# A graph attention layer on one core: edge ids worked beside the first k,v rows, and k,v split into bf16 pieces in PSUM

## The chip, the cores and the metric

The kernel runs on one core of one Trainium2 chip. Its time is the device time of one execution in microseconds (us), from the first to the last instruction and what lies around them; lower is better. In what follows PE is TensorE (the matmul engine), PEld its weight loads, DVE is VectorE, ACT is ScalarE, POOL is GpSimd, and SP is SyncE, which issues most DMAs. All of them run at once; each takes its own instructions strictly in order.

## The reference

One layer of graph attention with 12500 nodes and 412500 edges, sorted by destination `dst`, followed by two layer norms. With `q`, `k`, `v`, `h` linear in the node features and `eh` linear in the edge features:

```
attn_in = concat([q[src], k[tgt], eh])                      # src, tgt are the edge's two ends
hmid    = leaky_relu(attn_in @ A1 + b1);  scores = leaky_relu(hmid @ A2 + b2)
w       = softmax(scores.mean(-1), axis=0)                  # over all edges
out     = segment_sum(w[:, None] * v[tgt], src)
x       = layernorm(x + (gamma * layernorm(h + out) + beta))
```

A1 is folded into the weights of q, k and eh, so that an edge's hidden row is a sum of three rows.

## The kernel before

**Two streams.** The edges are taken in 403 groups of 1024 (8 tiles of 128), in the order of the sorted `dst`. Stream one, `make(p)`, turns each tile of 128 edges into 128 records of 260 floats: the k row plus the edge part, the v row, and the place of the edge's other end. A record is written to a table in DRAM (`rtab`), at the place that puts edges with like `src` together. Stream two, `sums_of`, reads blocks of that table back, computes scores, weights and weighted sums, and the tail of the program does the two norms (`closing`). The edges are cut into three parts (groups 0 to 73 are not yet followed by any sums; from group 74 on both streams run side by side).

**Making records.** For each group: two one-hot matrices on DVE (`onehots`, which writes `oh`, `few` and `ohd`), two small counts on PE (`count`), the records' places on DVE (`masked`, `places`, the last writes `idx`); then for each half group 4 tiles of matmuls into one PSUM tile `pkv` (`rows`, lines 931 and 936: the first picks k,v rows out of 128 rows `kvs`, the second adds the edge part), a copy by ACT to one of 6 buffers `rec` (`evacuate`, lines 946 and 947), and four indirect DMAs issued by POOL (line 958). A group is thus 8 such DMAs, and there are 3224 in all. The loads of a group stand four groups ahead in SP's queue (`load`, `load_ids`).

**The tables that this needs.** `kvs` comes from a DRAM table `kvtab`, where each of the 98 blocks of 128 node rows holds k and v as three bf16 pieces whose sum is the float32 value (s=0 is the value rounded to bf16, s=1 the rounded remainder, s=2 the remainder of that). The first 7 blocks (`NB`) are made at the start, the other 13 lots of 7 by the generator `tables()` in small steps between the steps of `make`; the same generator then makes 14 lots of q and h rows. A lot of k,v: a load of `xt`, 7 matmuls into PSUM tiles `ph`, 7 additions of the bias on DVE into an SBUF tile `ns` (line 1731), then `parts3`: ACT copies to bf16 (line 1694), DVE subtracts that copy from the float32 (line 1699), ACT, DVE, ACT; then one DMA to `kvtab`. The ids of the edges (`edges`: `dI`, `sI`; results `dtab`, `stab` and `start`, `blk`, `srcl`, `twin`) are made likewise in chunks: the first has 104 groups and is made at the start, the six others of up to 52 by the generator `later()`.

**What sets the order.** From `with tc.manual_schedule()` on the order is the one written: a loop over the steps `i` of `make` (6 to a group) takes a step of `tables()` whenever `made * n0 < i * nt` and one of `later()` whenever `sent * n0 < i * ne`. n0 is nine tenths of the steps of the first 74 groups (399), nt the number of steps that `tables()` has, ne that of `later()`. Before that point, the start, a list scheduler orders what the program has written. In the kernel before the start runs: weights (`first_layer`), the first k,v rows, their split (lines 628 and 631, all on DVE), the write to `kvtab` (line 633), and then the first chunk of ids, whose buffers come from a pool that is opened after the pool of the first rows is closed.

Of the kernel before, what the change touches and what calls it, by code (L numbers as in the profile page):

```python
# [10 lines left out]
FP = mybir.dt.float32  # L11
BF = mybir.dt.bfloat16
# [9 lines left out]
P = 128  # L22
D = 128
DE = 64
H = 8
# [356 lines left out]
def first_layer(nc, prep, pprep, WqT, WkT, WeT, Wv, Wn, A1, bq, bk, be, bv, bn, b1):  # L382

    A1s = prep.tile([D, 3, D], FP)
    nc.sync.dma_start(out=A1s, in_=A1.rearrange("(s k) d -> k s d", k=D))
    wT = prep.tile([D, 2, D], FP)
# [5 lines left out]
    cols = prep.tile([D, 3], FP)  # L392
    for i, b in enumerate((bq, bk, be)):
        nc.sync.dma_start(out=cols[:, i : i + 1], in_=b)
    W = prep.tile([D, 4, D], FP)
    nc.sync.dma_start(out=W[:, 2, :], in_=Wv)
    nc.sync.dma_start(out=W[:, 3, :], in_=Wn)
    bias = prep.tile([P, 4, D], FP)
    nc.vector.memset(bias[:, 1, :], 0.0)
    nc.sync.dma_start(out=bias[:, 2, :], in_=bv.to_broadcast([P, D]))  # L400
    nc.sync.dma_start(out=bias[:, 3, :], in_=bn.to_broadcast([P, D]))
    b1_b = prep.tile([P, D], FP)
    nc.sync.dma_start(out=b1_b, in_=b1.to_broadcast([P, D]))
# [68 lines left out]
def sorted_path(  # L472
# [39 lines left out]
    A2s = const.tile([D, 32], FP)  # L512
    nc.vector.memset(A2s, 0.0)
    nc.scalar.dma_start(out=A2s[:, :H], in_=A2)
    nc.vector.tensor_reduce(A2s[:, H : H + 1], A2s[:, :H], AX.X, ALU.add)
    for j, part in enumerate((1.0, -1.0)):
        nc.vector.tensor_scalar(
            A2s[:, H + 1 + j : H + 2 + j], A2s[:, H : H + 1], part * SLOPE / (1 - SLOPE), None,
            op0=ALU.mult,
        )  # L520
    nc.vector.memset(A2s[:, H : H + 1], 0.0)
    b2_r = const.tile([1, 32], FP)
    nc.vector.memset(b2_r, 0.0)
    nc.scalar.dma_start(out=b2_r[:, :H], in_=b2.rearrange("h o -> o h"))
    nc.vector.tensor_reduce(b2_r[:, H : H + 1], b2_r[:, :H], AX.X, ALU.add)
    for j, part in enumerate((1.0, -1.0)):
        nc.vector.tensor_scalar(
            b2_r[:, H + 1 + j : H + 2 + j], b2_r[:, H : H + 1], part * SLOPE / (1 - SLOPE), None,
            op0=ALU.mult,
        )  # L530
    nc.vector.memset(b2_r[:, H : H + 1], 0.0)
    b2_d = dram.tile([32, 1], FP, name="b2_d")
    nc.scalar.dma_start(out=b2_d.rearrange("h o -> o h"), in_=b2_r)
    b2_c = const.tile([P, 1], FP)
    headsum = const.tile([P, 4], FP)
    nc.vector.memset(headsum, 0.0)
    signs = const.tile([32, 1], FP)
    nc.gpsimd.memset(signs, 1 - SLOPE)
    nc.gpsimd.affine_select(
        out=signs, in_=signs, compare_op=ALU.not_equal, fill=SLOPE - 1, base=-(H + 2),  # L540
        pattern=[[0, 1]], channel_multiplier=1,
    )
    for j in range(4):
        nc.scalar.dma_start(out=b2_c[32 * j : 32 * j + 32, :], in_=b2_d)
        nc.vector.tensor_copy(headsum[32 * j : 32 * j + 32, j : j + 1], signs)


# [48 lines left out]
    def kv_product(xt, pool, j):  # L596
        pn = pool.tile([P, 4 * P], FP, name="ph")
        nc.tensor.matmul(
            pn[:, : 2 * D], xt[:, j, :], Wkv.rearrange("k s d -> k (s d)"), start=True, stop=True
        )  # L600
        return pn

    def kv_biased(ns, j, pn):
        nc.vector.tensor_add(
            ns[:, j, :, :], pn[:, : 2 * D].rearrange("p (s d) -> p s d", s=2), bias_kv
        )
# [5 lines left out]
    with tc.tile_pool(name="prep", bufs=1) as prep, tc.tile_pool(  # L612
        name="pprep", bufs=1, space=PSUM
    ) as pprep, tc.tile_pool(name="pnode", bufs=4, space=PSUM) as pnode:
        W, We_, bias = first_layer(
            nc, prep, pprep, WqT, WkT, WeT, Wv, Wn, A1, bq, bk, be, bv, bn, b1
        )
        nc.vector.tensor_copy(Wkv, W[:, 1:3, :])
        nc.vector.tensor_copy(bias_kv, bias[:, 1:3, :])
        xt = prep.tile([D, NB, P], FP, name="xt")  # L620
        nc.sync.dma_start(out=xt, in_=xN[:, 0, :, :])
        ns = prep.tile([P, NB, 2, D], FP, name="ns")
        for j in range(NB):
            kv_biased(ns, j, kv_product(xt, pnode, j))
        skv = prep.tile([P, NB, 3, 2, D], BF, name="skv")
        rest = ns
        for s in range(3):
            nc.vector.tensor_copy(skv[:, :, s, :, :], rest)
            if s < 2:
                less = prep.tile([P, NB, 2, D], FP, name=f"less{s}")  # L630
                nc.vector.tensor_tensor(less, rest, skv[:, :, s, :, :], op=ALU.subtract)
                rest = less
        nc.sync.dma_start(out=kv_rows(0), in_=skv.rearrange("p b s t d -> p (b s t d)"))
        nc.vector.memset(WeS, 0.0)
        for h in range(2):
            half = slice(h * DE, (h + 1) * DE)
            nc.vector.tensor_copy(WeS[half, h, :], We_[half, :])
        for to, of in ((Wqh, W), (bias_qh, bias)):
            nc.vector.tensor_copy(to, of[:, 0:4:3, :])

# [14 lines left out]
    def edges(tmp, c, size):  # L655
# [22 lines left out]
        yield  # L678
        nc.vector.tensor_reduce(mm[:m, 0, c : c + 1], dl[:m, :], AX.X, ALU.max)
        yield  # L680
        nc.vector.tensor_reduce(mm[:m, 1, c : c + 1], dl[:m, :], AX.X, ALU.min)
        nc.sync.dma_start(out=start[:, g0:g1], in_=stab[g0:g1, :].rearrange("g o -> o g"))
# [34 lines left out]
    with tc.tile_pool(name="tmp", bufs=1) as tmp:  # L717
        for _ in edges(tmp, 0, CH):
            pass

# [982 lines left out]
    def tables():  # L1703
# [10 lines left out]

        load_x(0)
        yield
        for i, (kv, g) in enumerate(jobs):
            load_x(i + 1)
            xt = xts.pop(i)
            ns = np_.tile([P, NB, 2, D], FP, name=f"ns{i % 2}")  # L1720
            w, bias = (Wkv, bias_kv) if kv else (Wqh, bias_qh)
            for j in range(NB + 1):
                before = ph if j else None
                if j < NB:
                    ph = php.tile([P, 4 * P], FP, name="ph")
                    nc.tensor.matmul(
                        ph[:, : 2 * D], xt[:, j, :], w.rearrange("k s d -> k (s d)"),
                        start=True, stop=True,
                    )
                if j:  # L1730
                    nc.vector.tensor_tensor(
                        ns[:, j - 1, :, :].rearrange("p s d -> p (s d)"), before[:, : 2 * D],
                        bias.rearrange("p s d -> p (s d)"), op=ALU.add,
                    )
                yield
            sp = np_.tile([P, NB, 3, 2, D], BF, name="sp")
            if kv:
                yield from parts3([sp[:, :, s, :, :] for s in range(3)], ns, 2)
                nc.sync.dma_start(
                    out=kv_rows(g), in_=sp.rearrange("p b s t d -> p (b s t d)")  # L1740
                )
                made_rows[0] = g + 1
            else:
                sq = np_.tile([P, NB, 2, 1, D], HF, name="sq")
                yield from powers(g, ns[:, :, 0, :])
                yield from parts3([sq[:, :, s, :, :] for s in range(2)], ns[:, :, 0:1, :], 1)
                bl = slice(g * NB, (g + 1) * NB)
                nc.sync.dma_start(out=htab[:, bl, :], in_=ns[:, :, 1, :])
                nc.sync.dma_start(
                    out=qtab[:, bl, :], in_=sq.rearrange("p b s o d -> p b (s o d)")  # L1750
                )
# [27 lines left out]
    with tc.manual_schedule():  # L1779
# [12 lines left out]
        tabs, made, nt = tables(), 0, 1 + (2 * ng - 1) * (NB + 7) + ng  # L1792
# [119 lines left out]
```

## Time and profile before

| | us |
|---|---|
| median of 3 runs | 4827.88 (4826.07 to 4830.85) |
| the profiled execution, whole time | 4829.19 |
| its span, first to last instruction | 4827.2 |
| first indirect DMA of a record starts | 59.30 |
| last one starts | 4282.75 |

The profile's page has a share of busy time by engine (DVE 84%, PE 83%, POOL 68%, ACT 65% over the span). These are averages over a start (to 59 us), a first stage in which only records and tables are made (to about 860), a long stage with both streams (to 4284), and a tail without records. So stages are read apart below. Rows of the group views have busy time in us and mean nanoseconds of one instruction after the first bar, and the idle time of the engine before them, with what ended it, after the second. Rows of the timeline begin with the start and the length in us. Rows of the windows give for a stretch its length, then busy time and the count of instructions, the granted clock of PE as a share, the busy share of the DMA engines and GB/s.

### The profile page before, as it was taken

How to read it: one execution, taken by the hardware profiler on the slowest of the kernel's cores; microseconds unless marked ns; L12 is line 12 of the kernel's file. 1: busy time of each engine (PE TensorE's matmuls, PEld its weight loads, DVE VectorE, ACT ScalarE, POOL GpSimd, SP SyncE). 2: the span in 40 equal slices, each digit the busy share in tenths (PEclk: the TensorE clock that was granted, in tenths of full speed). 3: DMA queues.
4: the chain of work that ended last, by engine and by line, in shares of the span. 5: the costliest groups of instructions: out<-in, count | busy, mean ns of one | idle time of the engine just before them, and what ended most of it. 6: DMA issues, size and time to landing. Idle time of an engine off the chain costs nothing. (4 is left out here: it accounts for less than half of the span.)

```text
span 4827.2 us, 84360 instructions
## 1 busy us (share of the span) xinstructions
PE 3991.6 (83%) x26680; PEld 3111.2 (64%) x26680; DVE 4064.7 (84%) x8217; ACT 3144.8 (65%) x8198; POOL 3304.4 (68%) x3279
## 2 busy tenths in 40 slices
PE   3556655577788999999999999998998899998997
PEld 2334433466666777777777666666777777666777
DVE  8878886688878999999998888888999988877767
ACT  2432222366666778787787777777777777777886
POOL 3777777777777777777777777777777777741103
PEclk7877785899888999999999999999999999999999
DMA  6888887888988999999999999999999999989964
GB/s 196 282 279 288 286 298 243 294 300 298 296 299 299 358 336 334 333 348 337 323 335 324 329 331 329 332 336 325 342 332 326 333 316 334 320 294 327 318 215 176
DMA packets 599153, 1484.41 MB, mean 308 GB/s; under 512 B 100352, under 2 KB 299923, under 8 KB 596902
## 3 DMA queue, kind: packets, MB, share of 16 engines
q1 hardware_dynamic: 436350, 1049.04, 65.4%
q0 software_dynamic: 154752, 429.39, 23.3%
q8 instruction: 212, 3.47, 0.3%
q14 instruction: 247, 2.02, 0.1%
q10 hardware_dynamic: 7592, 0.48, 0.1%
HBM read 906.61 MB, written 611.06 MB: 314 GB/s over the span
## 5 line engine op out<-in xcount | busy, mean ns | idle before, releaser
L958 POOL DMA_INDIRECT rtab<-rec,idx x3224 | 3219.2, 999 | 1061.2 <-issue 777.2
L946 ACT ACTIVATE rec<-pkv 128x1024 f32<-128x1024 f32 x806 | 822.2, 1020 | 1120.4 <-DMA rtab<-rec,idx 572.8
L1346 ACT ACTIVATE ohw<-ohs,w 128x128 f32<-128x128 bf16 x3626 | 1189.1, 399 | 75.7 <-DVE ohs L1332 27.2
L1375 PE MATMUL psm<-rt,ohw 128*128 128x128 f32 x7252 | 1023.1, 285 | 1.1 <-ACT ohw L1346 1.0
L1375 PEld LDWEIGHTS psm<-rt,ohw 128*128 128x128 f32 x7252 | 943.9, 197 | 76.1 <-ACT hm L1243 7.7
L936 PE MATMUL pkv<-WeS,eat 128*128 128x256 f32 x3224 | 946.4, 421 | 0.0
L1247 DVE TENSOR_TENSOR hm<-ph,hm 128x512 f32<-128x512 f32 (+1 forms) x949 | 627.4, 661 | 300.9 <-ACT hm L1243 299.0
L931 PE MATMUL pkv<-kvs,ohd 128*128 128x256 bf16 x3224 | 539.1, 295 | 373.6 <-ACT rec L946 370.2
L931 PEld LDWEIGHTS <-ohd 128*128 128x128 bf16 x3224 | 320.9, 105 | 645.9 <-issue 531.8
L936 PEld LDWEIGHTS pkv<-WeS,eat 128*128 128x128 f32 x3224 | 620.2, 214 | 75.0
L1224 PE MATMUL ph<-ident,rt 128*128 128x128 f32 x3626 | 587.2, 284 | 64.5 <-DVE hm L1247 63.6
L1210 DVE TENSOR_SCALAR ohT<-rowB,iotaP,power 128x512 bf16<-128x512 uint8 (+2 forms) x1274 | 598.9, 492 | 34.8 <-DMA rowB<-row 34.6
L1243 ACT ACTIVATE hm<-ph 128x512 f32<-128x512 f32 (+1 forms) x949 | 537.5, 566 | 84.1 <-PE ph L1233 29.2
L1224 PEld LDWEIGHTS ph<-ident,rt 128*128 128x128 f32 x3626 | 418.3, 146 | 269.7 <-issue 145.5
L1233 PE MATMUL ph<-ohT,qs 128*128 128x512 bf16 (+2 forms) x2548 | 559.7, 323 | 16.1 <-DVE ohT L1210 11.3
L872 DVE TENSOR_SCALAR ohd<-dstb,node 128x1152 bf16<-128x1152 uint8 x404 | 565.0, 1399 | 4.5 <-PE pkv L931 4.5
L900 DVE TENSOR_TENSOR ats<-pc,oh 128x792 f32<-128x792 f32 x403 | 392.2, 973 | 61.7 <-PE pc L880 56.6
L1332 DVE TENSOR_TENSOR ohs<-iotaE,sl 128x512 bf16<-128x512 bf16 (+1 forms) x949 | 404.6, 426 | 5.0 <-ACT ohw L1346 4.8
L862 DVE TENSOR_REDUCE few<-oh 128x99 bf16<-128x792 bf16 x403 | 395.1, 980 | 13.9
L911 DVE TENSOR_REDUCE pos<-ats 128x8 f32<-128x792 f32 x403 | 390.7, 970 | 2.5
L1258 PE MATMUL psc<-hm,A2s 128*32 128x512 f32 (+1 forms) x1898 | 345.9, 607 | 31.9 <-DVE hm L1247 23.7
L1284 PEld LDWEIGHTS psm<-headsum,z 96*128 96x128 f32 (+2 forms) x2112 | 259.7, 193 | 32.8 <-issue 8.3
(190 smaller groups left out, 3790.5 us busy)
## 6 DMA issues: line engine op xcount, KB each, us to landing
rt<-rtab SPq DMA_DIRECT2D x160, 1950.0 KB
rt<-rtab SPq DMA_DIRECT2D x96, 1560.0 KB
eat<-in_ea SPq DMA_DIRECT2D x201, 512.0 KB
rtab<-rec,idx POOLq DMA_INDIRECT x3224
dstb<-dtab SPq DMA_DIRECT2D x201, 256.0 KB
qs<-qtab SPq DMA_DIRECT2D x256, 192.0 KB
atab<-old SPq DMA_DIRECT2D x256, 192.0 KB
old<-atab SPq DMA_DIRECT2D x224, 192.0 KB
```

What stands on the lines that cost most here:

```text
L872: nc.vector.tensor_scalar(to, row[:, cols], node, None, op0=ALU.is_equal)
L931: nc.tensor.matmul(pk[:, i, h, :], ohd[t], kvs, start=(h == 0), stop=False,)
L936: nc.tensor.matmul(pk[:, i, :, :D], eat[:, (j + i) * P : (j + i + 1) * P], WeS, start=False, stop=True,)
L946: nc.scalar.activation(rec[:, :, :, : 2 * D], pk, AF.Copy)
L958: one_tile = nc.gpsimd.indirect_dma_start(out=rtab[p % TABS][:, :], out_offset=bass.IndirectOffsetOnAxis(ap=idxs[g][:, t : t + 1], axis=0) ...
L1210: nc.vector.tensor_scalar(st["oh"][k][:, (a - t0) * P : (b - t0) * P], st["rowB"][:, a * P : b * P], iotaP, power[:, bs[u] : bs[u] + 1], o ...
L1224: nc.tensor.matmul(ph[:, j * P : (j + 1) * P], st["rt"][:, t0 + j, :D], ident, is_transpose=True, start=(j == 0), stop=False,)
L1233: nc.tensor.matmul(ph[:, cols], st["qs"][:, j0 // t, s, :], oh[:, cols], start=False, stop=(s == 1 and j1 == t0 + n),)
L1243: nc.scalar.activation(hm, state[i]["ph", k][:, : n * P], AF.Copy, scale=SLOPE)
L1247: nc.vector.tensor_tensor(hm, ph[:, : n * P], hm, op=ALU.max)
L1346: nc.scalar.activation(ohw[:, j, :], ohs[:, :, j], AF.Copy, scale=st["w"][:, t0 + j : t0 + j + 1])
L1375: nc.tensor.matmul(st["psS"][:, (1 + u) * P : (2 + u) * P], ohw[:, j, :], st["rt"][:, t0 + j, D : 2 * D], start=(k == 0), stop=(k == t - 1),)
```

## The change

Four things, in one edit:

1. **The start in another order.** `edges` and its tiles are defined ahead of the first rows, the pools of both are open together, and the first chunk of ids now has 52 groups (so that seven more follow instead of six). Its loads `dI` and `sI` are the first DMAs of SP. Steps of it are interleaved with the first k,v rows. `first_layer` gives the three columns of biases and the three broadcast biases to ACT's DMA queue (`small`), and its loads are in another order.
2. **k,v split in PSUM.** New `kv_stages`: two blocks of 128 rows share one PSUM tile of 512 floats. `product` (PE), `biased` (DVE adds the bias within PSUM), `piece(0)` (ACT writes the bf16 piece from PSUM), `rest_of(0)` (PE adds minus that piece to the PSUM tile, by a bf16 matmul with minus the identity), `piece(1)`, `rest_of(1)`, `piece(2)`. It serves the first rows and the 13 other lots. DVE's copies and subtractions of lines 628, 631 and 1699 (for k,v) are gone, and so is ACT's one copy of 7 blocks at a time.
3. **Steps.** A new pair of blocks is begun every second step, and up to four pairs are under way. A lot of k,v takes 8 steps instead of 14. nt is 320 instead of 393, ne 77 instead of 66.
4. The PSUM tiles come by turns from the pools `ph` and `psm` (two buffers each; no sums run yet), and the pieces go to two SBUF tiles `sp0` and `sp1` instead of one.

The lots of q and h rows are made as before. The instructions after the first stage are the same and in the same order on all engines.

```diff
@@ first_layer(..., small=None)
+    small = small or nc.sync
     nc.sync.dma_start(out=A1s, in_=A1.rearrange("(s k) d -> k s d", k=D))
+        small.dma_start(out=cols[:, i : i + 1], in_=b)
+    nc.sync.dma_start(out=wT[:, 1, :], in_=WkT)
     nc.sync.dma_start(out=wT[:, 0, :], in_=WqT)
-    nc.sync.dma_start(out=wT[:, 1, :], in_=WkT)
+    small.dma_start(out=b1_b, in_=b1.to_broadcast([P, D]))
+    small.dma_start(out=bias[:, 2, :], in_=bv.to_broadcast([P, D]))
+    small.dma_start(out=bias[:, 3, :], in_=bn.to_broadcast([P, D]))
...
@@ sorted_path
+    def kv_stages(pool, name, xt, j, m, sp, minus):
+        own = {}
+        def product():
+            own["p"] = pool.tile([P, 4 * P], FP, name=name)
+            for i in range(m):
+                nc.tensor.matmul(
+                    own["p"][:, 2 * D * i : 2 * D * (i + 1)], xt[:, j + i, :],
+                    Wkv.rearrange("k s d -> k (s d)"), start=(i == 0), stop=(i == m - 1),
+                )
+        def biased():
+            pn = own["p"][:, : 2 * D * m].rearrange("p (b w) -> p b w", b=m)
+            nc.vector.tensor_tensor(
+                pn, pn,
+                bias_kv.rearrange("p (o s) d -> p o (s d)", o=1).to_broadcast([P, m, 2 * D]),
+                op=ALU.add,
+            )
+        def piece(k):
+            nc.scalar.activation(
+                sp[:, j : j + m, k, :, :],
+                own["p"][:, : 2 * D * m].rearrange("p (b s d) -> p b s d", b=m, s=2), AF.Copy,
+            )
+        def rest_of(k):
+            nc.tensor.matmul(
+                own["p"][:, : 2 * D * m], minus,
+                sp[:, j : j + m, k, :, :].rearrange("p b s d -> p b (s d)"),
+                start=False, stop=True, skip_group_check=True,
+            )
+        return [
+            product, biased, lambda: piece(0), lambda: rest_of(0), lambda: piece(1),
+            lambda: rest_of(1), lambda: piece(2),
+        ]
...
-    chunks = [(0, min(CH, G))] + [
-        (g, min(g + CH // 2, G)) for g in range(CH, G, CH // 2)
-    ]
+    chunks = [(g, min(g + CH // 2, G)) for g in range(0, G, CH // 2)]
...
+        ids_of = edges(tmp, 0, CH // 2)
+        next(ids_of)
...
+        nc.sync.dma_start(out=xt, in_=xN[:, 0, :, :])
+        next(ids_of)
...
+        for s in range(2 * len(tiles) + 5):
+            for k, stages in enumerate(tiles):
+                if 0 <= s - 2 * k < len(stages):
+                    stages[s - 2 * k]()
+            next(ids_of, None)
+        nc.sync.dma_start(out=kv_rows(0), in_=skv.rearrange("p b s t d -> p (b s t d)"))
...
@@ tables
+        flying, per = {}, -(-NB // 2)
+        for s in range(2 * per * (ng - 1) + 5):
+            k, odd = divmod(s, 2)
+            i, j = divmod(k, per)
+            if not odd and i < ng - 1:
+                if j == 0:
+                    load_x(i + 1)
+                    sp = np_.tile([P, NB, 3, 2, D], BF, name=f"sp{i % 2}")
+                flying[k] = sp, kv_stages(
+                    *((php, "ph"), (psmp, "psm"))[k // 2 % 2], xts[i], 2 * j, min(2, NB - 2 * j), sp, minus
+                )
+            for k in sorted(flying):
+                of, stages = flying[k]
+                stages[s - 2 * k]()
...
-            if kv:
-                yield from parts3([sp[:, :, s, :, :] for s in range(3)], ns, 2)
...
-        tabs, made, nt = tables(), 0, 1 + (2 * ng - 1) * (NB + 7) + ng
+        tabs, made, nt = tables(), 0, 6 + 2 * (ng - 1) * -(-NB // 2) + ng * (NB + 8)
```

How the instructions move, at three places. The first is SP's queue at the start, before: the first rows go to `kvtab` (line 633) ahead of the first ids (`dI`, `sI`), and `zeros`, a block of zeros that later fills unused places of the tables, goes out before group 0's loads (`dstb`, `eat`, and next `kvs`).

```order
L621 DMA xt_177<-in_xN 128x896
L1020 DMA firsts_382<-in_bounds 3x99
L633 DMA kvtab_65<-skv_201 128x5376
L660 DMA dI_230<-in_dst_g 104x1024
L663 DMA sI_232<-in_src 128x832
L556 DMA zeros_125<-empty_377 128x1040
L672 DMA dtab_78<-db_236 104x1024
L677 DMA stab_79<-row_241 104x1
L838 DMA dstb_384<-dtab_78 128x2048
L682 DMA start_224<-stab_79 1x104
L818 DMA eat_386<-in_ea 128x1024
```

The same queue in the changed kernel, from the read of group 0's ids on.

```order
L864 DMA dstb_392<-dtab_78 128x2048
L638 DMA start_106<-stab_79 1x52
L844 DMA eat_394<-in_ea 128x1024
L702 DMA kvtab_65<-skv_175 128x5376
L848 TENSOR_LOAD start_106
L853 ISA
L853 DMA kvs_399<-kvtab_65 128x256
L848 TENSOR_LOAD start_106
L853 ISA
L853 DMA kvs_404<-kvtab_65 128x256
L864 DMA dstb_406<-dtab_78 128x2048
L521 DMA zeros_93<-empty_385 128x1040
```

The ids are done ahead of the write to `kvtab` now, and `zeros` has moved behind the first two loads of `kvs` and ahead of all loads of groups 2 and up; its source `empty` is filled by DVE after the one-hots of group 1.

The second place is DVE in the first lot of k,v that `tables()` makes, before: each subtraction of line 1699 runs over 7 blocks at once (1792 floats), between the work on two groups.

```order
L911 TENSOR_REDUCE pos_581<-ats_566 128x8
L913 SCALAR_TENSOR_TENSOR idx_583<-pos_581,twin_223 128x8
L1699 TENSOR_TENSOR less0_585<-ns0_468,sp_568 128x1792
L851 TENSOR_TENSOR oh_603<-blk_221,iotaE_87 128x792
L862 TENSOR_REDUCE few_605<-oh_603 128x99
L872 TENSOR_SCALAR ohd_607<-dstb_398,node_281 128x3x384
L1699 TENSOR_TENSOR less1_609<-less0_585,sp_568 128x1792
```

DVE in the changed kernel, at about the same groups: line 575 is the addition of the bias within PSUM.

```order
L898 TENSOR_SCALAR ohd_543<-dstb_406,node_289 128x3x384
L575 TENSOR_TENSOR psm_547<-psm_547,hm_99 128x512
L926 TENSOR_TENSOR ats_578<-pc_426,oh_539 128x792
L575 TENSOR_TENSOR psm_569<-psm_569,hm_99 128x256
L937 TENSOR_REDUCE pos_594<-ats_578 128x8
L939 SCALAR_TENSOR_TENSOR idx_596<-pos_594,twin_105 128x8
```

Of k,v only that addition is left on DVE, four for each lot.

The third place is PE in the same lot of the changed kernel, between the records' matmuls of one half group (line 962) and those of the next (line 957): a product of two blocks (line 568, `hm` is the weight) and two subtractions by `minus` (line 588) of two other pairs.

```order
L962 MATMUL pkv_531<-WeS_94,eat_394 128x2x128 x2
L906 LDWEIGHTS rest_299
L906 MATMUL pc_426<-few_453,rest_299 128x99
L568 MATMUL psm_547<-hm_99,xt_459 128x256 x2
L588 LDWEIGHTS minus_457
L588 MATMUL ph_479<-sp0_478,minus_457 128x512
L588 LDWEIGHTS minus_457
L588 MATMUL ph_494<-sp0_478,minus_457 128x512
L906 LDWEIGHTS above_296
L906 MATMUL pc_426<-few_541,above_296 128x99
L568 MATMUL psm_569<-hm_99,xt_459 128x256
L957 LDWEIGHTS ohd_455
```

Before, PE had only products of one block each there; now it also has the subtractions, each of which waits for ACT's piece of the same pair.

More of the change, by code (lines that the diff above doesn't have):

```diff
@@ L510, in sorted_path @@
     nc.vector.memset(eps, EPS)
[L512 to L545, printed above, removed]
     fmax = max(plan.tiles[k] - plan.cap // P + max(plan.fill[k]) for k in range(TABS))
@@ L608, in kv_rows @@
     def kv_rows(c):
         return kvtab[c * NB * P : (c + 1) * NB * P, :].rearrange("(p b) w -> p (b w)", p=P)
[L612 to L639, printed above, removed]
@@ new lines, in sorted_path @@
+    A2s = const.tile([D, 32], FP)
+    nc.vector.memset(A2s, 0.0)
+    nc.scalar.dma_start(out=A2s[:, :H], in_=A2)
+    nc.vector.tensor_reduce(A2s[:, H : H + 1], A2s[:, :H], AX.X, ALU.add)
+    for j, part in enumerate((1.0, -1.0)):
+        nc.vector.tensor_scalar(
+            A2s[:, H + 1 + j : H + 2 + j], A2s[:, H : H + 1], part * SLOPE / (1 - SLOPE), None,
+            op0=ALU.mult,
+        )
+    nc.vector.memset(A2s[:, H : H + 1], 0.0)
+    b2_r = const.tile([1, 32], FP)
+    nc.vector.memset(b2_r, 0.0)
```

119 lines of the change are left out of this document (77 added, 42 removed).

## The prediction

> **What bounds the kernel now.** I read the groups first, then windows of POOL alone by stage, then POOL's waits, then the timeline of the start and of some long record DMAs. Times are of the profiled execution (4829.19 us, 1.31 above the median of the runs); the sum is made against it and then lowered by that 1.3.
>
> ```profile
> L958 POOL DMA_INDIRECT rtab<-rec,idx x3224 | 3219.2, 999 | 1061.2 <-issue 777.2
> ...
> core 0: us, POOL busy (x), PEclk, DMA share, GB/s
> 68.60:386.00 317.40, 249.24 (x224) 0.78 0.85 279
> 386.00:860.00 474.00, 362.87 (x362) 0.70 0.83 273
> 860.00:1560.00 700.00, 534.82 (x543) 0.88 0.89 303
> ...
> 2160.00:3200.00 1040.00, 794.36 (x806) 0.97 0.95 331
> ...
> POOL rtab L958 <- ACT rec L947: 21.9, 45, 2.5
> ```
>
> POOL is busy for only two thirds of the span and still sets the pace: its record DMAs follow each other almost without a real wait. One takes 700.00/543 = 1.289 us from 860 to 1560 and 1.290 from 2160 to 3200, though the DMA engines and PE's clock differ there, and most of the idle time before them is put down to "issue", which waits for nothing. The last row, from the waits between 860 and 4300, is what POOL waited for ACT's copies: 21.9 us in 45 pieces. So a record stream that reaches 860 earlier ends the kernel earlier by as much: from there on every engine has the same instructions in the same order and is tied to the stream by the record buffers.
>
> Two stretches are off that pace: all before the first record, and 68.6 to 386, where the lots of k,v are made and a record takes 317.40/224 = 1.417 us.
>
> **The start.** The rows that carry it:
>
> ```profile
> 7.07 0.43 SPq L621 DMA_DIRECT2D xt<-in_xN  x1
> 12.15 5.08 PE L598 MATMUL ph<-hm,xt 128*128 128x256 f32 x14 [4.95 <-DMA xt<-in_xN]
> 28.00 0.37 SPq L633 DMA_DIRECT2D kvtab<-skv  x1
> 32.75 0.34 SPq L660 DMA_DIRECT2D dI<-in_dst_g  x1
> 33.49 0.93 DVE L555 MEMSET empty<- 128x1040 f32 x1 [0.17 <-issue]
> 37.34 0.15 DVE L666 TENSOR_SCALAR first<-dI 104x1 f32<-104x1 int32 x1 [2.92 <-DMA dI<-in_dst_g]
> 48.71 1.23 SPq L827 DMA_DIRECT2D kvs<-kvtab  x2
> 50.66 1.01 PE L931 MATMUL pkv<-kvs,ohd 128*128 128x256 bf16 x4 [1.86 <-DVE tw L714]
> 51.47 1.91 PE L936 MATMUL pkv<-WeS,eat 128*128 128x256 f32 x4
> 54.34 0.21 ACT L947 ACTIVATE rec<-srcl 128x16 f32<-128x16 uint8 x1
> 54.70 1.40 SPq L1711 DMA_DIRECT2D xt<-in_xN  x1
> 58.24 0.17 DVE L913 SCALAR_TENSOR_TENSOR idx<-pos,twin 128x8 int32<-128x8 f32 x1
> 59.30 1.16 POOL L958 DMA_INDIRECT rtab<-rec,idx  x1 [56.02 <-DVE oh L851]
> 59.81 1.40 DVE L872 TENSOR_SCALAR ohd<-dstb,node 128x1152 bf16<-128x1152 uint8 x1
> 62.39 1.22 PE L1726 MATMUL ph<-hm,xt 128*128 128x256 f32 x2 [8.93 <-DMA xt<-in_xN]
> 68.65 1.19 POOL L958 DMA_INDIRECT rtab<-rec,idx  x1 [4.40 <-DVE ns L1731]
> ...
> L1247 DVE TENSOR_TENSOR hm<-ph,hm 128x512 f32<-128x512 f32 x784 | 537.3, 685 | 262.4 <-ACT hm L1243 260.8
> L1243 ACT ACTIVATE hm<-ph 128x512 f32<-128x512 f32 x784 | 458.0, 584 | 33.1 <-PE ph L1233 19.8 <-ACT slT L1188 6.8 <-PE psm L1375 2.4
> L1233 PE MATMUL ph<-ohT,qs 128*128 128x512 bf16 x918 | 278.8, 386 | 16.1 <-DVE ohT L1210 11.3 <-DMA atab<-old 4.8
> ```
>
> The chain was: products, split on DVE, write to `kvtab` issued at 28.00, its landing (only then does `dI` go out, 4.75 us later), 21.1 us of id work (37.34 to 58.41), first record at 59.30. Of these, after the change:
>
> - First products: `xt` is still the tenth load or so on SP (two id loads ahead of it, six small loads gone to ACT's idle queue). I leave them at 12.3. Between 11 and 15.
> - The split: the seven products take 5.1 us as before (to 17.4). ACT writes nine pieces of 512 (584 ns) and three of 256 (0.36 us, on the line from 584 ns to the 1691 that 1792 floats take, below), 6.3 us, and PE eight subtractions, none above 386 ns. They alternate within a pair, four pairs under way. ACT can start after the second product and one addition (14.7), so at the earliest it ends at 21.0; if the whole 6.3 and half of PE's 3.1 come after the last product, at 25.3. I take 24.0 for the write to `kvtab`, 4.0 earlier.
> - Landing as before, 4.75 us: `kvs` of group 0 goes out at 29 instead of 48.71. The ids are no longer in between: the first chunk of 52 groups, which I take at half of 21.1, runs on DVE while the weights and products are waited for. With group 0's own one-hots and places I count `idx` ready at 33 (27 to 37).
> - From `kvs` to the filled record buffer took 5.84 us (48.71 to 54.55): 35. So the first record starts at 35, 24 earlier.
> - But only four of them. The next half group stands in PE's queue behind a product that needs the lot's `xt`. SP issued that load 6.0 us after `kvs`; now `zeros` is in between, and it waits for DVE's fill of `empty`, which follows group 1's one-hots: 33 + 2.8 (58.41 to 61.21) + 0.9, about 37. Then 0.3 for its own issue, the 4.3 us that SP took from 50.42 to 54.70, 7.7 to the landing of `xt` (62.39) and 6.3 to the fifth record: 55.6 instead of 68.65. **Gain 13.0**; 20 if `zeros` costs nothing, 8 if DVE or the split is 5 us later.
>
> The first records' own gain of 24 is thus half given back: what is late next is `xt`.
>
> **The subtractions on DVE.**
>
> ```profile
> 121.51 2.02 DVE L1699 TENSOR_TENSOR less<-less,sp 128x1792 f32<-128x1792 f32 x1
> 121.89 2.47 POOL L958 DMA_INDIRECT rtab<-rec,idx  x1 [0.30 <-issue]
> ...
> 128.57 0.96 POOL L958 DMA_INDIRECT rtab<-rec,idx  x1 [0.30 <-issue]
> 128.93 0.42 DVE L1731 TENSOR_TENSOR ns<-ph,hm 128x256 f32<-128x256 f32 x1
> ...
> 59.30:386.00 326.70, 52.55 (x26) 0.77 0.84 277
> ```
>
> A record DMA that meets a subtraction takes 2.47 us instead of 0.96: it ends 0.83 after the subtraction does. One that meets the addition of the bias, with one operand in PSUM, takes its 0.96. The last row is a window of line 1699 alone on DVE: up to 386 it holds 26 instructions, two for each of 13 lots, 52.55 us. POOL's stretch from 68.6 to 386 loses 224 x (1.417 - 1.289) = 28.7 us against the steady pace, 1.1 us for each of them. The change takes all 26 out. The new addition reads PSUM and one SBUF operand like the one that cost nothing, but writes PSUM, which no row shows: between nothing and, if its output held POOL as a subtraction does, 52 x 1.1 x 0.685/2.02 = 19 us. I take nothing, by the row at 128.57, the nearest. **Gain 28.7**, between 24 (a sixth is other contention) and 32 (the same count against 0.96 + 0.30).
>
> The Trainium skill, SBUF — State Buffer, section Who interferes with whom, speaks against this term: it says that a VectorE instruction with two SBUF inputs takes only the read side of the port pair shared with GpSimd, while descriptors need the write side (marked there as inferred), and that `tensor_tensor` was not seen to stall DMAs. The row at 121.89 does not agree. The same section says that one SBUF input does not contend, and there the row at 128.57 agrees.
>
> **What comes on top, and what hides it.** In the stage of the lots:
>
> ```profile
> core 0: us, PE busy (x) PEld busy (x) DVE busy (x) ACT busy (x) POOL busy (x), PEclk, DMA share, GB/s
> 59.30:386.00 326.70, 186.59 (x733) 129.34 (x734) 262.34 (x381) 129.82 (x159) 253.27 (x228) 0.77 0.84 277
> ...
> L936 PE MATMUL pkv<-WeS,eat 128*128 128x256 f32 x608 | 232.1, 522 | 0.0
> L1726 PE MATMUL ph<-hm,xt 128*128 128x256 f32 x378 | 141.3, 486 | 45.4 <-DVE ns L1731 34.9 <-DMA xt<-in_xN 8.9 <-DVE first L666 1.0
> L931 PE MATMUL pkv<-kvs,ohd 128*128 128x256 bf16 x608 | 125.8, 346 | 264.6 <-ACT rec L946 263.3 <-DMA rtab<-empty 1.2
> L946 ACT ACTIVATE rec<-pkv 128x1024 f32<-128x1024 f32 x151 | 154.2, 1021 | 482.0 <-DMA rtab<-rec,idx 353.3 <-PE pkv L936 71.1 <-PE pc L880 35.0
> L1694 ACT ACTIVATE sp<-ns 128x1792 bf16<-128x1792 f32 x13 | 22.0, 1691 | 5.1 <-DVE ns L1731 2.6 <-ACT rec L947 1.5 <-issue 1.0
> ```
>
> The lots now end after 109 of 320 steps, at step 136 of `make`, 45 half groups in. POOL takes 4 x 1.289 = 5.16 us for a half group.
>
> - ACT: a lot cost 3 x 1.69 = 5.1 us and now 6.3: 13 lots, 82 us over 45 half groups, 1.8 each, beside 1.23 for the record's copies. Hidden: it waits 353 us in this stage for POOL to free record buffers.
> - DVE: the additions (13 x (3 x 0.685 + 0.42) = 32 us for 91 x 0.42 = 38) and seven id chunks for six (10.5 more) against 52.6 us of subtractions gone. Hidden: DVE was 80% busy and is less so.
> - PE: a lot has 7 products of 0.75 and 8 subtractions of at most 0.39, 8.3 us; over 45 half groups 2.4 each, beside (232.1 + 125.8)/151 = 2.4 for the record's own. 4.8 of 5.16, at this stage's clock of 0.77. Hidden, though not by much; if that cover goes, see the second rival.
> - SP: the write of a lot to `kvtab` now stands right behind its last piece, every 10 steps instead of 14; loads have four groups of lead. Nothing. The lots of q are spread wider, with 14 subtractions as before: nothing, give or take 3.
>
> Sum: 4829.2 - 13.0 - 28.7 = 4787.5, less 1.3 for the median: **4786 us**.
>
> **Rivals.**
>
> *The long record DMAs are not the subtractions' doing.* Then only the start gains: 4829.2 - 13.0 - 1.3 = 4815. For it: the one stretch is also where `kvtab` and `xt` transfers are thickest. Against: the overlap above, and the return to 1.309 (474.00/362) right after the lots. This is what the page's rule above would give. 5%.
>
> *The record's chain becomes the bound (slower than before).* Within a lot PE's subtraction waits for ACT's piece, ACT's next piece for PE, and the record's matmuls and copies stand between them in both queues; `pkv` has one buffer. If PE's work and the copy add up, at the slow rate of the first half group (1.01 and 1.91, 2.72 from 50.66 to 53.38), a half group takes 2.72 + 2.4 x 2.72/2.37 + 1.02 = 6.5 us instead of 5.16: 45 x 1.34 = 60, giving 4846. It decides from 6.3 us on (4838). For it: PE's share above. Against: ACT's 353 us of waiting says that this chain runs ahead of POOL, and the clock rises where PE is denser (0.77 here, 0.88 and 0.97 in the later windows). 12%: 5% beyond 4838, 7% between 4818 and that.
>
> *The start gains nothing that lasts*: the fifth record is as late as before, since `xt` and the fills wait in a fuller queue. 4829.2 - 28.7 - 1.3 = 4799. 10%.
>
> **How the numbers follow.** The forecast has 73%, with its own range from 4827.9 - 20 - 32 = 4776 to 4827.9 - 8 - 24 = 4796. The range for 8 in 10 goes down to 4766 (the start's full 24 and 32, and a few us from the lots of q) and up to 4816, which takes in the first and the third rival; only the second, and the ends of the forecast's tails, are left out. About 0.2% (9.7 us) can be told from no change here. Faster by more: 73 + 5 + 10, 88%; same: the milder part of the second rival, 7%; slower 5%.
>
> **What would show it.** First record near 35 us and the fifth near 56, with `zeros` issued near 37 and PE waiting for `xt`. From the fifth record to about 290 us, no record DMAs of 1.9 us and more, and some 1.29 us for each. ACT still waiting for record buffers in that stretch. The record stream done about 41 us earlier (near 4241) and the tail unchanged at 544 us. Wrong would be: POOL waiting for ACT's copies in the first 300 us, record DMAs still stretched (then beside the additions in PSUM, or with no partner on DVE), or a stream that starts early and stalls again before 100 us.

## The result and the profile after

The median went from 4826.98 to 4792.53 us (ratio 0.9927, 95% interval 0.9910 to 0.9944). The profiled execution took 4788.9 us, 3.6 below its median, where the one of before was 2.2 above its own: their spans differ by 40.0 us (4827.2 and 4787.2), the medians by 34.5. The lines below are of the profile after; line 984 is now the record's DMA, 972 and 973 are ACT's copies, 568, 575, 582 and 588 are product, bias, piece and subtraction of k,v.

The start, from the timeline (start and length in us, then engine and line, idle time before it and what ended that in brackets):

```profile
13.90 1.62 PE L568 MATMUL ph<-hm,xt 128*128 128x256 f32 x3 [1.95 <-DVE q L649]
25.61 0.36 SPq L702 DMA_DIRECT2D kvtab<-skv  x1
30.27 1.22 SPq L853 DMA_DIRECT2D kvs<-kvtab  x2
31.26 0.17 DVE L939 SCALAR_TENSOR_TENSOR idx<-pos,twin 128x8 int32<-128x8 f32 x1
35.41 0.33 SPq L521 DMA_DIRECT2D zeros<-empty  x1
36.38 1.16 POOL L984 DMA_INDIRECT rtab<-rec,idx  x1 [33.11 <-ACT rec L973]
41.02 0.75 SPq L1737 DMA_DIRECT2D xt<-in_xN  x1
48.12 2.08 PE L568 MATMUL ph<-hm,xt 128*128 128x256 f32 x4 [13.17 <-DMA xt<-in_xN]
54.28 0.95 POOL L984 DMA_INDIRECT rtab<-rec,idx  x1 [12.95 <-ACT rec L973]
```

The first record starts 22.9 us earlier (59.30 before), the fifth only 14.4 (68.65 before). Between them POOL stands 12.95 us: PE stands 13.17 us for the `xt` that SP issued after `zeros`.

POOL alone by windows (length, busy time and count, PE's clock, DMA share, GB/s); the first one runs from the fifth record to record 229, which is the 224 records of the window from 68.60 to 386.00 before:

```profile
54.20:348.20 294.00, 220.51 (x224) 0.83 0.96 315
348.20:825.00 476.80, 360.03 (x361) 0.73 0.82 265
825.00:1525.00 700.00, 534.51 (x544) 0.90 0.89 304
2130.00:3170.00 1040.00, 794.98 (x805) 0.98 0.95 331
```

The 224 records take 294.0 us, 1.3125 each, for 1.417. The later windows are as before (1.287 and 1.292 for a record; 476.80/361 = 1.321 in the second). POOL's busy time in the first fell by 28.7 us, from 249.24 to 220.51: no record DMA there takes 1.9 us any more, where 23 did.

Where the gain stands at some records, counted in the order of POOL's DMAs (start times in us from the traces):

| record | before | after | gained |
|---|---|---|---|
| 1 | 59.30 | 36.38 | 22.9 |
| 5 | 68.65 | 54.28 | 14.4 |
| 229 | 387.25 | 348.27 | 39.0 |
| 593 | 864.68 | 829.95 | 34.7 |
| 3224, the last | 4282.75 | 4246.92 | 35.8 |
| end of the span | 4827.2 | 4787.2 | 40.0 |

### The profile page after: what moved, and what is told of

Its sections match the earlier page's. It is cut to its first block, busy times and chain, and to the rows that moved or that the text cites. A ratio compares the mean times of both kernels' runs of the same rounds, so it can differ in the third digit from the quotient of the medians.

```text
span 4787.2 us, 84477 instructions
## 1 busy us (share of the span) xinstructions
PE 3944.9 (82%) x26529; PEld 3095.7 (65%) x26792; DVE 4005.4 (84%) x8175; ACT 3157.1 (66%) x8327; POOL 3275.1 (68%) x3279
## 5 line engine op out<-in xcount | busy, mean ns | idle before, releaser
L962 PE MATMUL pkv<-WeS,eat 128*128 128x256 f32 x3224 | 926.8, 414 | 0.0
L957 PE MATMUL pkv<-kvs,ohd 128*128 128x256 bf16 x3224 | 527.2, 290 | 330.4 <-ACT rec L972 313.5
L962 PEld LDWEIGHTS pkv<-WeS,eat 128*128 128x128 f32 x3224 | 607.4, 210 | 70.3
L1259 PE MATMUL ph<-ohT,qs 128*128 128x512 bf16 (+3 forms) x2285 | 500.7, 315 | 24.6 <-DVE ohT L1236 11.6
```

What stands on the lines that cost most here:

```text
L957: nc.tensor.matmul(pk[:, i, h, :], ohd[t], kvs, start=(h == 0), stop=False,)
L962: nc.tensor.matmul(pk[:, i, :, :D], eat[:, (j + i) * P : (j + i + 1) * P], WeS, start=False, stop=True,)
L1259: nc.tensor.matmul(ph[:, cols], st["qs"][:, j0 // t, s, :], oh[:, cols], start=False, stop=(s == 1 and j1 == t0 + n),)
```

## The experiments

The twelve runs fell on three chips: e1 to e4 on the first, e5 to e8 on the second, e9 to e12 on the third. The kernel before took 4832.67 us on the first, 5774.42 on the second and 4834.68 on the third, and each ratio is to the kernel before on the run's own chip. On the second, POOL waited again and again where it doesn't on the others (see the last section), so its times are compared only among themselves, and its traces used for the durations of single instructions. "Stretch" is the time from the fifth record to record 229; "long" counts the record DMAs of 1.3 us and more in it. The changed kernel's own stretch was 294.0 in its first trace and 296.5 in e12, so a difference of 2 or 3 us between two stretches says nothing.

| kernel | fifth record | stretch | long | median | ratio to before (95%) |
|---|---|---|---|---|---|
| before | 68.65 | 318.6 | 28 | 4826.98 | |
| after | 54.28 | 294.0 | 4 | 4792.53 | 0.9927 (0.9910 to 0.9944) |
| e1_start_only | 54.21 | 321.4 | 25 | 4820.48 | 0.9973 (0.9961 to 0.9985) |
| e2_lots_only | 69.20 | 298.0 | 4 | 4806.11 | 0.9944 (0.9926 to 0.9963) |
| e3_sub_back | 55.06 | 325.2 | 27 | 4826.47 | 0.9979 (0.9967 to 0.9991) |
| e4_one_input | 53.63 | 308.7 | 28 | 4810.20 | 0.9958 (0.9942 to 0.9975) |
| e5_xt_early (second chip) | 46.25 | 340.6 | 3 | 5750.77 | 0.9958 (0.9944 to 0.9972) |
| e6_one_input_slow (second chip) | 55.30 | 340.8 | 4 | 5762.99 | 0.9977 (0.9964 to 0.9991) |
| e7_after_again (second chip) | 58.30 | 337.2 | 1 | 5761.97 | 0.9974 (0.9959 to 0.9989) |
| e8_q_too (second chip) | 47.71 | 340.2 | 2 | 5758.48 | 0.9975 (0.9961 to 0.9988) |
| e9_dve_in_psum | 55.16 | 298.9 | 6 | 4799.51 | 0.9928 (0.9915 to 0.9941) |
| e10_xt_early_again | 42.11 | 303.4 | 8 | 4795.28 | 0.9914 (0.9901 to 0.9927) |
| e11_q_too_again | 44.12 | 297.5 | 2 | 4787.18 | 0.9899 (0.9884 to 0.9913) |
| e12_after_beside | 54.30 | 296.5 | 5 | 4801.28 | 0.9930 (0.9917 to 0.9942) |

### The two halves of the change, each alone

```diff
 # e1_start_only: the changed kernel, with tables() of before
-                flying[k] = sp, kv_stages(...)
+                yield from parts3([sp[:, :, s, :, :] for s in range(3)], ns, 2)
 # e2_lots_only: the kernel before, with tables() and kv_stages of the changed one
-                yield from parts3([sp[:, :, s, :, :] for s in range(3)], ns, 2)
+                flying[k] = sp, kv_stages(...)
```

> The new start (first ids of 52 groups beside the first rows, first rows split in PSUM) with the 13 later k,v lots made and split as before, on DVE. Theory (start and subtractions add up, each by itself): first record at 36.4 us, fifth at about 54, so 14 us earlier than before, and about 20 record DMAs of 1.9 us and more between the fifth record and the end of the k,v lots; 4827 - 14 = 4813 (4808 to 4818). Rival (what the start gains is lost again in the stretch of the lots, because another wait sets the pace there): 4824 to 4830. Rival (the gain is all the start's): 4793.

> The start as before, but the 13 later k,v lots split in PSUM. Theory: first record at 59.3, fifth at 68.7 us as before; no record DMA of 1.9 us or more from there to the end of the k,v lots; about 24.6 us gained by record 229, the same as that stretch gained in the changed kernel: 4827 - 25 = 4802 (4797 to 4808). Rival (the stretch is slow for its transfers and not for the subtractions): 4827 +- 4, long record DMAs still there.

Measured: the start alone brings the fifth record to 54.21 and keeps the long DMAs (19 of 1.9 us and more), 12.2 us by the medians, 13.0 by the ratio, for the 14 that were expected. (Its median lies 2.5 above the expected range, but on this chip the kernel before is 5.7 us slower too.) The lots alone leave the first and fifth record at 59.77 and 69.20, cut the stretch by 20.6 us, and give 26.6. The two halves add up to 38.8, with the 34.5 of the whole inside the intervals. Neither is the doing of the other.

### What makes a record DMA long

```diff
+            if i < ng - 1 and s - 2 * per * i in (2, 6):       # 26 times, in the later k,v lots
+                nc.vector.tensor_tensor(extra, one_in, two_in, op=ALU.subtract)           # e3
+                nc.vector.tensor_scalar(extra, one_in, eps, None, op0=ALU.add)            # e4: 1792 flat
+                nc.vector.tensor_scalar(extra[:, :, :560], one_in, eps, None, op0=ALU.add) # e6: 3 x 560
```

> The changed kernel with two extra subtractions on DVE in each k,v lot (26 in all; f32 minus bf16 to f32, 128x1792, all three in SBUF, as the removed ones were), whose result nobody reads and which wait for nothing. Theory (the two-input SBUF subtraction stretches POOL's record DMAs): each of them 2.0 us on DVE, the record DMA beside it about 2.5 us again, 1.1 us each: 4792.5 + 26 x 1.1 = 4821 (4814 to 4826). Rival (the long record DMAs came from the transfers or from waits around the lots): record DMAs stay at 0.96, time 4790 to 4797.

> The changed kernel with 26 extra one-input instructions on DVE at the same places (tensor_scalar, uint8 to bf16, 128x1792, like the one that makes ohd, 1.40 us for 1152), result unread. Theory (it is the two SBUF inputs, not DVE's time): about 2.2 us each on DVE, record DMAs beside them stay at 0.96, time 4790 to 4798. Rival (any long DVE instruction at these places delays the records, through the port or by making the places and one-hots late): 4810 to 4825.

> As e4_one_input, but in rows of 560 to an output with a gap (128x1680 in three rows, as the instruction that makes ohd is laid out), so that DVE takes one element for each of its cycles: 26 instructions of about 2.0 us, one SBUF input, result unread. Theory (what holds POOL is a second SBUF stream of DVE, by two inputs or by its double pace, not DVE's time): record DMAs beside them 0.96, no more than 5 of 1.3 us and more up to record 229, 0 to 6 us above the changed kernel. Rival (any long DVE instruction at these places): 20 or more stretched records, 15 to 29 us above it.

One place of each from the timelines of e3, e4 and e6, the extra instruction on DVE with the record DMAs beside it:

```profile
158.51 2.01 DVE L1755 TENSOR_TENSOR extra<-one_in,two_in 128x1792 f32<-128x1792 f32 x1
158.56 2.79 POOL L984 DMA_INDIRECT rtab<-rec,idx  x1 [0.30 <-issue]
161.66 0.96 POOL L984 DMA_INDIRECT rtab<-rec,idx  x1 [0.31 <-issue]
```

```profile
172.34 1.14 DVE L1753 TENSOR_SCALAR extra<-one_in,eps 128x1792 bf16<-128x1792 uint8 x1
172.49 1.82 POOL L984 DMA_INDIRECT rtab<-rec,idx  x1 [0.30 <-issue]
174.62 0.96 POOL L984 DMA_INDIRECT rtab<-rec,idx  x1 [0.31 <-issue]
```

```profile
160.03 1.96 DVE L1753 TENSOR_SCALAR extra<-one_in,eps 128x1680 bf16<-128x1680 uint8 x1
160.81 0.96 POOL L984 DMA_INDIRECT rtab<-rec,idx  x1 [0.30 <-issue]
162.07 0.96 POOL L984 DMA_INDIRECT rtab<-rec,idx  x1 [0.31 <-issue]
```

In each of these fences the first record DMA begins while DVE works. Beside the subtraction it ends 0.83 us after it (at 161.35 and 160.52), as in the kernel before. The 26 subtractions, whose result nobody reads, lengthen the stretch by 31.2 us over the changed kernel's (325.2 against 294.0). By the ratios, 0.9979 against 0.9930, they cost some 24 us at the end, where the theory had 28.6; the median of 4826.47 lies 0.5 above the expected range, on the same chip as e1's.

e4 missed. Its instruction has one input, yet 28 long DMAs came, the rival's mark. But it took 1.14 us for the 2.2 expected: 0.64 ns for an element, where line 898 with the same types takes 1.40 us for 1152, 1.22 ns. DVE ran it at about double pace. So the theory had to be mended: not two inputs alone hold POOL; DVE at its double pace does too. The stretch grew by 14.7 us. e6 is the control: the same types and engine, a longer time (1.95 us, 1.16 ns for an element), and a layout that DVE takes at its single pace. There the long DMAs are 4 (the changed kernel has 1 on that chip and 4 in its first trace), none of them beside the extra instruction: a record DMA that overlaps it takes 0.963 us (the mean of 51), 0.98 at most. DVE's time is not what stretches. Its median of 5762.99 stands beside 5761.97 for the changed kernel on that chip.

> The changed kernel, but DVE subtracts the pieces in place in PSUM (one operand in PSUM, the piece in SBUF, 128x512, about 0.7 us) where PE subtracted them: 104 such instructions in the later lots, some 64 us of DVE, more than the 52.6 us of the old subtractions. Theory (it is the second SBUF input that holds POOL): record DMAs beside them stay at 0.96, no more than 5 of 1.3 us and more up to record 229; but DVE, 181 of 246 us busy there in the changed kernel, becomes full, so POOL may wait for idx: 0 to 15 us above the changed kernel. Rival (the gain came from taking the subtractions off DVE, wherever its operands are): record DMAs stretched again, 20 us and more above it.

```diff
-                nc.tensor.matmul(own["p"][...], minus, sp[:, j : j + m, k, :, :]..., start=False, ...)
+                nc.vector.tensor_tensor(pn, pn, sp[:, j : j + m, k, :, :]..., op=ALU.subtract)
```

One such subtraction in e9's timeline, with the record DMA that begins beside it:

```profile
122.45 0.70 DVE L589 TENSOR_TENSOR ph<-ph,sp 128x512 f32<-128x512 f32 x1 [0.27 <-ACT sp L582]
122.81 0.96 POOL L984 DMA_INDIRECT rtab<-rec,idx  x1 [0.30 <-issue]
```

Here DVE does the subtractions again, but out of PSUM: 104 of them in the later lots, 0.42 to 0.70 us each, and DVE is 227.70 of 246 us busy from 54 to 300. The record DMAs that overlap them by more than 0.2 us take 0.974 us (mean of 59). In the whole stretch 6 are long, one more than expected, and the kernel takes 4799.51 us beside 4801.28 for the changed one. (The pieces are also shorter here than the old subtractions of 2.02 us. That is not what saves them: the one-hots of line 877, of 0.56 us with two inputs in SBUF, do stretch record DMAs; see the last section.) So of the two things that the change did to a subtraction, giving it to TensorE and leaving its operand in PSUM, the second carries the whole gain; DVE's 46 us more cost nothing that can be seen.

### What is late next at the start

```diff
-    empties(np_)          # stood further up
...
+    tabs = tables()
+    next(tabs)            # loads xt of the first later lot
+    empties(np_)          # fills empty, writes zeros
     with tc.manual_schedule():
```

> The changed kernel with the xt of the first later lot loaded right behind the write to kvtab, ahead of kvs and zeros; nothing else. Theory (the fifth record waits for that xt, behind zeros in SP's queue): the 12.95 us that POOL waits between the fourth and the fifth record shrink to about 2, the fifth record starts at 42 to 45 us for 54.3, and the gain stays to the end: 10 to 12 us below the changed kernel, about 46 below the kernel before. Rival (the next wait stands right behind it: kvs or the one-hots of group 1, or DVE): fifth record after 50, within 4 us of the changed kernel.

> The changed kernel once more, to compare with the others on one chip: 33 to 37 us below the kernel before (ratio 0.9927).

> e5_xt_early once more, on another chip if it falls so, beside the changed kernel: fifth record at 42 to 45 us, 10 to 12 us below the changed kernel at the end, ratio to the kernel before 0.9904. Rival: the gain is lost again by the end, within 4 us of the changed kernel.

> The changed kernel beside the three others: ratio 0.9927 to the kernel before, 33 to 37 us.

The fifth record came to 46.25 us for 58.30 in e7 on the second chip, to 42.11 for 54.30 in e12 on the third: the 12 us of waiting for `xt` are gone, and the fifth record follows the fourth after the usual 0.30 us. At the end e5 is 11.2 us below e7 (5750.77 and 5761.97). On the third chip it is 6.0 (4795.28 and 4801.28), where 10 to 12 were expected. The intervals overlap on both chips, and in the third chip's profiles nothing is left of the gain by record 381 (556.00 and 555.86). So the place is shown, and what it brings at the end is not settled. (e7 itself gave 0.9974 for the expected 0.9927, on the chip of the long waits; e12 gave 0.9930.) Two waits in the trace of e10 show what is late after `xt`, the first on DVE, the other on ACT, each with the record that follows:

```profile
48.06 0.15 DVE L625 TENSOR_SCALAR first<-dI 52x1 f32<-52x1 int32 x1 [7.53 <-DMA dI<-in_dst_g]
56.49 0.96 POOL L984 DMA_INDIRECT rtab<-rec,idx  x1 [4.13 <-ACT rec L973]
...
223.46 0.60 ACT L582 ACTIVATE sp<-ph 128x512 bf16<-128x512 f32 x1 [13.56 <-DMA kvtab<-sp]
228.70 0.96 POOL L984 DMA_INDIRECT rtab<-rec,idx  x1 [4.02 <-ACT rec L973]
```

DVE stands for the second chunk of ids, with the next group's one-hots behind it; ACT stands for the write of an older lot to `kvtab`, with the record's copy behind it.

### The same cure for the lots of q

```diff
-        nc.vector.tensor_tensor(q, q, inv..., op=ALU.mult)
+        for j in range(NB):
+            nc.scalar.activation(q[:, j, :], q[:, j, :], AF.Copy, scale=inv[:, j : j + 1])
...
-                nc.vector.tensor_tensor(less, rest, to[s], op=ALU.subtract)
+            nc.tensor.matmul(ph[:, : m * D], minus, to[0][:, j : j + m, :], start=True, stop=True)
+            nc.vector.tensor_tensor(less[:, j : j + m, :], rest[:, j : j + m, :], ph..., op=ALU.add)
```

> e5_xt_early, and the two DVE instructions with two SBUF inputs that each q lot has are taken out too: the product with inverse is made by ACT, a block at a time, and the first piece is subtracted by DVE from an operand that PE wrote to PSUM. Theory: of the 17 record DMAs of 1.3 us and more between records 229 and 593 at most 6 stay, 5 to 10 us gained there over e5_xt_early. Rival (those come from transfers or from the id chunks): 14 or more stay, 0 to 2 us.

> e8_q_too once more: no more than 6 record DMAs of 1.3 us and more between records 229 and 593, as in its first run, and where POOL sets the pace 5 to 10 us gained there over the kernel with xt early alone, ratio to the kernel before 0.989. Rival (POOL then waits elsewhere, for ACT or DMAs, as in its first run): 0 to 2 us.

The q lot's subtraction in the changed kernel, and the two halves that stand for it in e11, whose second operand is in PSUM:

```profile
331.25 1.09 DVE L1725 TENSOR_TENSOR less<-ns,sq 128x896 f32<-128x896 f32 x1 [1.07 <-ACT sq L1720]
331.32 1.85 POOL L984 DMA_INDIRECT rtab<-rec,idx  x1 [0.30 <-ACT sq L1720]
```

```profile
330.11 1.15 DVE L1725 TENSOR_TENSOR less<-ns,ph 128x512 f32<-128x512 f32 x2 [1.70 <-PE ph L1722]
330.15 0.96 POOL L984 DMA_INDIRECT rtab<-rec,idx  x1 [0.50 <-issue]
```

Between records 229 and 593 the long DMAs went from 17 (in e5) to 5 in e8 on the second chip, where it brought no time (5758.48 and 5750.77, for the 5 to 10 us expected to be gained). On the third chip they went from 22 to 8, two more than expected, and those 364 records took 478.5 us against 488.5 in e10; but in e12, with the q lots as in e10, they took 482.6, so 4 to 10 us of it may be the q lots'. With 4787.18 us e11 is 8.1 below e10 and 14.1 below the changed kernel on the same chip; its ratio, 0.9899 (0.9884 to 0.9913), lies wholly under that of the changed kernel beside it (0.9917 to 0.9942). By the median it is the fastest version here; its interval overlaps that of e10.

## Why the prediction was right

The time came out 6.5 us above the forecast, inside the range. By its steps:

- **Start, 13.0: measured 14.4.** The products began at 13.90 for 12.3, the write to `kvtab` at 25.61 for 24.0, `kvs` at 30.27 for 29, `idx` at 31.26 for 33, `zeros` at 35.41 for 37, the first record at 36.38 for 35 and the fifth at 54.28 for 55.6. PE did wait for `xt`, as it says, and e10 shows that nothing else held the fifth record.
- **Subtractions, 28.7: measured 29.6** as time in record DMAs (above 0.96 us for each, the 224 records of the stretch had 35.1 us before and 5.5 after); e3 puts them back for 31.2. The unknown price, a DVE addition that writes PSUM, is nothing: the 40 record DMAs that overlap line 575 by more than 0.2 us between 54 and 290 us took 0.960 us on the mean. (The prediction's upper end of 32 is a slip: 224 records against 0.96 + 0.30 give 35.)
- **What lies beside other work, 0: it cost 5.1 in the stretch.** This is the step that failed. The prediction has for SP's write of a lot to `kvtab` "Nothing", and for ACT "it waits 353 us in this stage for POOL to free record buffers". That row counts all 151 half groups up to 860 us; in the stretch of the lots the wait was a third of it. The record's copy by ACT in the groups of before (69 to 386 us), then its copy and its pieces in those of after (54 to 300):

```profile
L946 ACT ACTIVATE rec<-pkv 128x1024 f32<-128x1024 f32 x59 | 60.2, 1020 | 154.4 <-DMA rtab<-rec,idx 122.1 <-PE pkv L936 16.7 <-issue 13.7
```

```profile
L972 ACT ACTIVATE rec<-pkv 128x1024 f32<-128x1024 f32 x49 | 50.1, 1022 | 43.7 <-PE pkv L962 23.4 <-issue 12.8 <-DMA rtab<-rec,idx 4.2
L582 ACT ACTIVATE sp<-ph 128x512 bf16<-128x512 f32 x77 | 43.5, 598 | 53.0 <-DMA kvtab<-sp 42.3 <-DVE ph L575 7.7 <-PE ph L588 2.8
```

Ahead of its copies ACT waited 122.1 us for record buffers before and 4.2 after; now it waits 42.3 us ahead of its pieces for the landing of a lot's write, since `sp0` and `sp1` are two and the third lot's first piece must wait for the first lot's DMA. The record's copy stands behind that piece in ACT's queue, and some of it comes through to POOL. Its largest waits in the stretch:

```profile
70.66 0.95 POOL L984 DMA_INDIRECT rtab<-rec,idx  x1 [1.46 <-DVE idx L939]
...
249.54 0.96 POOL L984 DMA_INDIRECT rtab<-rec,idx  x1 [1.23 <-DMA rtab<-rec,idx]
...
261.43 0.60 ACT L582 ACTIVATE sp<-ph 128x512 bf16<-128x512 f32 x1 [3.78 <-DMA kvtab<-sp]
263.32 1.14 POOL L984 DMA_INDIRECT rtab<-rec,idx  x1 [2.36 <-ACT sp L582]
```

Beyond the 0.30 us between two record DMAs POOL waited 0.3 us in the stretch before and 5.4 after. 29.6 - 5.1 is, but for the rounding, the 24.6 that the stretch gained. Of the 5.4, 2.1 are the wait behind ACT's piece at 263.32, 1.2 the one for `idx`, and 1.4 two for the landing of an earlier record DMA (the DMA engines were 0.96 busy in this stretch, for 0.85 before); what made those landings late is not known. In e12 the wait at the same record behind ACT's piece is 3.5 of 6.8. So ACT's queue accounts for about half of the loss. The prediction looked at how long ACT's instructions take and not at what they would wait for: a buffer that a DMA still reads. A third `sp` buffer would test this; it wasn't tried, so this cause is read from the trace and not shown by a run.
- **Lots of q, "give or take 3": 4.3 lost** between records 229 and 593, most of it one wait of 4.0 us beyond the usual 0.30, at 549.58 us. Waits of 1.8 to 3.8 us stand at the same record or the next in e3, e4, e9 and e12; e2 has none there, e1 one of 1.8 four records later. In most of these the trace puts the wait down to the landing of an earlier record DMA; what it waits for is open.
- **After that, nothing: +1.1** up to the last record and +4.2 in the tail (540.2 us for 544.4). The tail of the other kernels on the first and third chip took 541.0 to 545.8 with the same instructions in it, so these 4.2 are not the change's. That the profile's 40.0 comes so near to the forecast 41.7 is in part luck: without them the change gained 35.8 there, near the 34.5 of the medians. (The two profiled executions differ by 40.3 us in whole time; one lies 2.2 above its median and the other 3.6 below, and that makes the rest.)

The rivals. That the long DMAs were not the subtractions' doing is refuted by e3. The Trainium skill, SBUF — State Buffer, section Who interferes with whom, infers that `tensor_tensor` with two SBUF inputs leaves descriptor generation alone, and lets it contend only with a GpSimd instruction that reads SBUF. e3's row at 158.56 (2.79 us for 0.96) shows that it doesn't leave this DMA alone; the DMA's instruction reads `idx` in SBUF, and whether that reading is what is held no run here tells. That the record's chain becomes the bound came nearer than the prediction's "ACT still waiting for record buffers" allowed, with 4.2 us left of 122.1; but a half group took 294.0/56 = 5.25 us and not 6.3, and PE, counted at 4.8 us for a half group, was busy 159.14 of the 246 us from 54 to 300, 3.4 for each. The start that gains nothing that lasts is refuted by e1.

## What to carry to other kernels

Where GpSimd issues the DMAs that set the pace, look at which DVE instructions its long ones overlap, and count their SBUF inputs: putting one operand of a two-input instruction in PSUM frees GpSimd even if DVE gets more to do (e9; e11 for the lots of q). A one-input instruction matters too where DVE runs it at double pace (e4, e6). More microseconds on an engine off the path cost nothing by themselves (e6, e9), until its queue holds a wait in front of what the path needs. So for each instruction that is moved into such a queue, ask also which buffer it writes and which DMA must have read that buffer.

## What the runs showed of the hardware

- A one-input DVE instruction of flat layout (uint8 to bf16, 128x1792) ran at 0.64 ns for an element and held POOL's record DMAs as a subtraction does: 26 of 1.15 us on the mean added 17.3 us to the record DMAs of the stretch (22.8 for 5.5 above 0.96), 0.67 each. In three rows of 560 it ran at 1.16 ns and held nothing. The Trainium skill says the first of these in SBUF — State Buffer, section Who interferes with whom: `tensor_scalar` in a two-port mode can take the port pair that DVE shares with GpSimd. The runs agree as far as they go: they show the pace and the hold, not the ports.
- A record DMA that begins beside such an instruction ends 0.83 us after it (158.51 + 2.01 and 158.56 + 2.79; 172.34 + 1.14 and 172.49 + 1.82), whatever the length of the instruction: 25 of 26 beside line 1699 before, all 24 in e3, all 12 beside line 1725 after end 0.83 or 0.84 us after it. So 0.83 of the 0.96 us come after the hold. Short instructions with two SBUF inputs hold too: beside the one-hot of line 877 (0.56 us) record DMAs of the changed kernel take up to 1.33 us and end 0.83 after it.
- One chip ran both kernels a fifth slower with record DMAs of the same length (0.98 us on the mean): from record 601 to 3000 of e7 there are 314 gaps of over 1 us between record DMAs, 899 us in all, and none in the changed kernel's first trace. Before 141 of them, 447 us, POOL waited for ACT's copy of a record, and from 1000 to 4600 us ACT waited 440 us ahead of those copies for something that the trace doesn't name. The other engines don't stand meanwhile: in the 241 gaps of over 2.5 us PE, ACT and DVE are busy for 52 to 60% of the time. The mean granted clock was 0.869, for 0.931. What made the gaps is not known.
